# A graph network on one core: messages in 32-column steps, one aggregation matmul per edge attribute, and one product for what a transpose leaves over

## The chip, the cores and the metric

The kernel runs on one core of a Trainium2 chip. The metric is the device time of one execution in microseconds (us). All arithmetic is in 32-bit floats. Each core has a TensorE (PE in the profile), a VectorE (DVE), a ScalarE (ACT), a GpSimd (POOL) and a SyncE (SP), and DMA queues that these engines fill. In this kernel GpSimd issues the gathers of node rows by index, SyncE issues the plain loads, and ScalarE issues the stores of finished node blocks.

## The reference, cut to what matters

Two layers of a graph network run over N = 6250 nodes and E = 200000 edges. A node has 160 features: 64 scalars and 32 vectors of three components. Edges are sorted by the node they end at (`dst`); early nodes have many more edges than late ones.

```python
# layer 0 (w: 192 weights an edge, from 10 inputs an edge; g: the mixed source node's row)
weight = silu(edge_length_embedded @ W_fc1) @ W_fc2
w0, w1, w2, w3 = weight[:, :64], weight[:, 64:128], weight[:, 128:160], weight[:, 160:]
gs, gv = x1s[edge_src], x1v[edge_src]            # 64 scalars; 32 vectors
e_s, e_v = edge_attr[:, :1], edge_attr[:, 1:]    # 4 attributes an edge: 1 + 3
mid0a = w0 * gs * e_s                            # 64
mid0b = w3 * einsum('euc,ec->eu', gv, e_v) / sqrt(3)      # 32
mid1a = w1[:, :, None] * gs[:, :, None] * e_v[:, None, :] # 64 x 3
mid1b = w2[:, :, None] * gv * e_s[:, :, None]             # 32 x 3
agg = segment_sum(concatenate([mid0a, mid0b, mid1a, mid1b]), edge_dst) / 4
# then linear maps of each node's sums, a residual and a layer norm

# layer 1 (w: 224 weights an edge, from 64 inputs an edge)
m_s1 = w1 * es * e0                              # 64
m_s2 = w4 * einsum('eci,ei->ec', ev, e1) / sqrt(3)        # 32
m_v1 = (w2 * es)[:, :, None] * e1[:, None, :]             # 64 x 3
m_v2 = w3[:, :, None] * ev * e0[:, :, None]               # 32 x 3
m_v3 = w5[:, :, None] * cross(ev, e1[:, None, :]) / sqrt(2) # 32 x 3
# segment sums as above, linear maps, silu and gates, a residual and a layer norm
```

Every message is a product of a weight, a gathered feature and one of four edge attributes. So a node's sum can be taken attribute by attribute: for each attribute the products of weights and features (`mid` in the kernel) are multiplied from the left by a matrix that has the attribute in the row of the edge and the column of its node (`sel`).

## The kernel before

**Tiles, groups and units.** 200000 edges are 1563 tiles of 128; two tiles are a pair (782), four a unit (391). Tiles are gathered into 284 groups of 3 to 12, such that the nodes at which a group's edges end lie in a window of 32. One loop over units runs for each layer, in `windows(i, loads, work)`. It is pipelined by hand: in step `u` it issues the gathers of unit `u + 4`, the weights and products of unit `u + 2`, the hidden layer of unit `u + 3`, and the aggregation of unit `u`. TensorE keeps this order as written (`keep_in_program_order`, in the helpers `matmul` and `transpose`, lines 134 and 139, under which every TensorE instruction shows in the profile). The other engines' orders are chosen by a scheduler from the same program.

**Steps of a unit.**
- `gather` (L665): one indirect DMA a tile on GpSimd brings 128 rows of 160 columns from `table` into `g`. A tile of `g` holds a pair, and there are 8 of them. `src`, the indices, and `ea`, the edge attributes, are loaded by SyncE for 48 tiles at a time (L578, L579).
- `inputs` and `hidden`: SyncE loads the edge inputs `e`, in layer 0 for 4 tiles at a time into one of three fixed buffers `e0` to `e2`, in layer 1 for 8 tiles at a time into one of two buffers `e`. TensorE makes `pa` (one matmul of 512 columns in layer 0, of 256 columns in layer 1), ScalarE turns it into `h`.
- `weights`: TensorE makes `pw` from `h`, one matmul a tile. There are three `pw` buffers in PSUM, a pair in each.
- `places` (L699): VectorE makes `sel`, 4 times 32 columns a tile.
- `products` (L681, L686): VectorE multiplies `pw` by `g` into `mid`. A pair takes one operation of 256 elements a partition for the scalars, and one of 192 for each kind of vector message (two in layer 0, three in layer 1). The messages of a tile lie in 320 columns in layer 0, and 416 in layer 1.
- `aggregate`: TensorE adds `sel` times `mid` to `pg`, a PSUM tile with a band of 32 partitions for each of the four attributes. A list `sums` says which columns of `mid` go to which band. In layer 0 there are six matmuls a tile (160, 96, 64, 64, 32 and 32 columns), so that the bands hold 160, 96, 96 and 96 columns. In layer 1 there are seven (160, 64, 96, 128, 96, 64 and 32), and every band holds 160.
- After a group's last tile ScalarE copies `pg` to `r` (L728, L730). One unit later `turn(g)` has TensorE transpose `r` into `pt`, of which there is one buffer, and VectorE adds `pt` to the group's window of `sm` (L749) and `sr` (L751). In layer 1 the 32 columns of `r` beyond 128 are turned by four matmuls of 32 columns against slices of the identity `ident`, ahead of the transpose of the other 128.

**Node blocks.** 49 blocks of 128 nodes are worked on as soon as their groups are turned: `prepare` and `proceed` put one step of such a block into a unit (`second_nodes` in layer 0, `last_nodes` in layer 1). Their matmuls go to `pn`, a PSUM tile with one buffer: the sums in `sm` and `sr` times weights `rm0`, `rr0` in layer 0, `rm1`, `rr1` in layer 1. In layer 1 three of these five matmuls are 96 columns wide, for the attributes 1 to 3. A block of layer 0 ends with four matmuls for layer 1's input, two of them 32 columns wide against `whoz`. Layer 0's blocks write the `table` of layer 1, and `xself` and `xmid`, which layer 1's blocks read back on SyncE.

**Prologue.** Ahead of both layers the kernel loads the nodes, writes layer 0's `table`, subtracts each group's first node from `dst`, and checks that the windows hold (otherwise a slower path, `general`, would run; it does not run with these inputs). It also fills the combined weights: `rm0` with copies on VectorE, `rm1` and `rr1` with 16 loads on SyncE.

Of the kernel before, what the change touches and what calls it, by code (L numbers as in the profile page):

```python
# [86 lines left out]
def kernel(ctx: ExitStack, tc: tile.TileContext, a, out):  # L87
# [17 lines left out]

    nc = tc.nc
# [68 lines left out]
    nc.gpsimd.dma_start(nv[:tail_n, NB - 1, :], a["nv_tail"])  # L175

# [192 lines left out]
    for j in range(2):  # L369
# [3 lines left out]
        for k in range(2):  # L373
# [5 lines left out]
    nc.vector.tensor_copy(rm0[0:64, 1:4, :, S:],  # L379
                          q[0:64, None, :, S:].to_broadcast([64, 3, 2, V]))  # L380
    nc.vector.tensor_copy(rm0[64:96, 1:4, :, 0:S],
                          q[64:96, None, :, 0:S].to_broadcast([32, 3, 2, S]))
# [10 lines left out]
    for at, n, f in ((0, 160, 0.125), (160, 32, r3 / 8), (192, 32, r2 / 8)):  # L393
# [4 lines left out]
    pieces = [(rm1[0:64, 0, ss], l2s[0:64]), (rm1[64:96, 0, vx], l2v[64:96]),  # L398
              (rm1[96:128, 0, vy], l2v[64:96]), (rr1[0:32, vz], l2v[64:96])]
    pieces += [(rr1[32 * c:32 * c + 32, ss], l2s[64:96]) for c in (1, 2, 3)]  # L400
    pieces += [(rm1[0:64, 1 + c, v], l2v[0:64]) for c, v in enumerate((vx, vy, vz))]

    for c, v0, v1 in ((1, vz, vy), (2, vz, vx), (3, vy, vx)):
        pieces += [(rm1[64:96, c, v0], l2v[96:128]), (rm1[96:128, c, v1], l2v[96:128])]
# [3 lines left out]
    for o, f in ((rm1[:, :, 0:96], fs), (rm1[:, :, 96:], fv), (rr1[:, 0:96], fs),  # L408
                 (rr1[:, 96:], fv), (rm1[64:96, 1, vz], -1.0), (rm1[96:128, 2, vx], -1.0),
                 (rm1[64:96, 3, vy], -1.0)):  # L410
        nc.vector.tensor_scalar(o, o, f, None, op0=OP.mult)
# [95 lines left out]
    def last_nodes(b, work, clear):  # L507
# [10 lines left out]
        def summed():  # L518
# [5 lines left out]
            for c in (1, 2, 3):  # L524
                matmul(q[:, 96:192], sm[:, c, rows], rm1[:, c, 96:192], start=False, stop=(c == 3))
# [20 lines left out]
    def windows(i, loads, work):  # L546
        nw = (192, 224)[i]

        at_c, at_d, at_f, at_a, at_b, wid = ((0, 64, None, 160, 224, 320),
                                             (0, 160, 64, 256, 320, 416))[i]  # L550

        if i == 0:
            sums = [(0, at_a, 0, 1, 160, 0), (1, 0, 0, 1, 96, 0), (2, 0, 0, 1, 64, 0),
                    (3, 0, 0, 1, 64, 0), (2, at_d + V, 0, 1, V, 64), (3, at_d + 2 * V, 0, 1, V, 64)]
        else:
            sums = [(0, at_a, 0, 1, 160, 0), (1, 0, 0, 1, 64, 0), (2, 0, 0, 1, 96, 0),
                    (3, 0, 0, 1, 128, 0), (1, at_f + V, 0, 1, 96, 64),
                    (2, at_f + 2 * V, 2 * V, 2, V, 96), (3, at_d + 2 * V, 0, 1, V, 128)]
        made = {}
        ec = (EC // 2, EC)[i]  # L560

        inputs_of = None
        if i == 0:

            inputs_of = [loads.tile([P, EC * P // 2], F32, name=f"e{k}", bufs=1) for k in range(3)]
            for e in inputs_of:
                nc.vector.memset(e, 0.0)
# [24 lines left out]
        def inputs(c):  # L592

            e0 = c * ec * P
            n = min(ec * P, E - e0)
            if i == 0:
                e = inputs_of[c % 3]
                nc.sync.dma_start(e[:10, :n], a["e10"][:, e0:e0 + n])
            else:

                e = loads.tile([P, EC * P // 2], F32, name="e", bufs=2)
# [68 lines left out]
        def products(p):  # L670

            m = min(2, NT - 2 * p)
            n = P if m == 2 else edges_of(2 * p)
            mid = work.tile([P, 2, 416], F32, name="mid", bufs=6)
            q, g = made["w", p], made["g", p]
            o = mid[:n, :m, :wid]
            gs = g[:n, :m, None, 0:S].to_broadcast([n, m, 2, S])
            gv = g[:n, :m, S:D].rearrange("p j (c d) -> p j c d", c=3)
            two = bass.AP(tensor=o.tensor, offset=o.offset,
                          ap=[o.ap[0], o.ap[1], [at_a, 2], [1, S]])  # L680
            nc.vector.tensor_tensor(  # L681
                two, q[:n, :m, 0:2 * S].rearrange("p j (k d) -> p j k d", k=2), gs, OP.mult)
            for w0, at in ((128, at_b), (160, at_d), (192, at_f)):
                if at is None:
                    continue
                nc.vector.tensor_tensor(  # L686
                    o[:, :, at:at + 96].rearrange("p j (c d) -> p j c d", c=3), gv,
                    q[:n, :m, None, w0:w0 + V].to_broadcast([n, m, 3, V]), OP.mult)
            made["m", p] = mid
# [19 lines left out]
        def aggregate(t):  # L709
# [6 lines left out]

            for q, (c, c0, step, k, w, at) in enumerate(sums):
                opens = first and not any(x[0] == c for x in sums[:q])
                closes = last and not any(x[0] == c for x in sums[q + 1:])
                o = mid[:n, t % 2, c0:c0 + w]  # L720
                if k > 1:
                    o = bass.AP(tensor=o.tensor, offset=o.offset, ap=[o.ap[0], [step, k], [1, w]])
                matmul(pg[32 * c:32 * c + 32, at:at + k * w], s[:n, t % 2, c, :], o,
                                 start=opens, stop=closes, tile_position=(0, 32 * c))
            if last:
                r = work.tile([P, 160], F32, name="r")
                w = (96, 160)[i]
                nc.scalar.activation(r[:, :w], pg[:, :w], AF.Copy)  # L728
                if i == 0:
                    nc.scalar.activation(r[:32, 96:], pg[:32, 96:160], AF.Copy)  # L730
                made["r", g] = r

        def turn(g):
# [5 lines left out]
            else:  # L739
                for c in range(4):  # L740
# [249 lines left out]
```

## Time and profile before

| | |
|---|---|
| median of 3 runs | 4143.48 us (4136.02 to 4146.3) |
| the profiled execution | 4137.19 us, of which the profile's span is 4135.4 us |
| granted clock of TensorE, mean | 0.911 |
| TensorE (PE) busy, matmuls | 3570.4 us, 86%, 53817 instructions |
| TensorE weight loads (PEld) | 2582.1 us, 62% |
| VectorE (DVE) busy | 2959.6 us, 72%, 10845 instructions |
| GpSimd (POOL) busy | 3013.5 us, 73%, 3232 instructions |
| ScalarE (ACT) busy | 947.6 us, 23%, 2386 instructions |
| layer 0, from its first gather to the end of its last | 66.9 to 2089.8 us |
| layer 1, the same | 2137.4 to 4101.3 us |

A busy share is an average over both layers, the prologue and the seam between the layers. A matmul's end is modelled, so the busy time of TensorE contains overlap of matmuls in its pipeline. A float32 matmul appears as two instructions, its two passes, each with a weight load of its own (PEld), which runs beside the matmul ahead of it. The rows of a profile name an instruction by source line, engine, operation and tiles; "idle before" is the time in which the engine stood still just ahead of it, with what ended the wait.

### The profile page before, as it was taken

The page shows a single profiled execution, that of the slowest core. Times are in us where ns is not written, and L with a number is a line of the kernel's source. Part 1 is how long each engine was busy: PE and PEld are TensorE (multiplying, and loading weights), DVE is VectorE, ACT ScalarE, POOL GpSimd, SP SyncE. Part 2 cuts the span into 40 slices and gives each one's busy share as a digit, 9 for nine tenths or more (in the row PEclk, how much of TensorE's full clock was granted, in tenths as well). Part 3 has the DMA queues.
Part 4 walks back from the last instruction along what each step waited for, and adds up shares of the span by engine and source line. Part 5 has one row for each costly group of instructions (what it writes and reads, how often), then busy time and mean ns, then how long its engine had stood idle before and what let it go on. Part 6 is the DMA issues. An engine that isn't in the chain of part 4 may idle for free.

```text
span 4135.4 us, 137335 instructions
## 1 busy us (share of the span) xinstructions
PE 3570.4 (86%) x53817; PEld 2582.1 (62%) x53817; DVE 2959.6 (72%) x10845; ACT 947.6 (23%) x2386; POOL 3013.5 (73%) x3232
## 2 busy tenths in 40 slices
PE   7878888889999999999988888888888788888877
PEld 5555566566666666666666666666666566666655
DVE  6766666667677777677657777777777777778887
ACT  2111111222223333333320011111112122222233
POOL 4777777777777777776637777777777777777775
PEclk8999999999999999999988888888898899888898
DMA  4222222332333333322223333333333333333432
GB/s 131 72 73 77 75 78 76 80 80 79 82 82 83 85 81 85 83 79 78 76 60 96 92 101 100 98 97 102 101 97 106 101 105 105 105 105 99 111 107 71
DMA packets 301525, 371.47 MB, mean 90 GB/s; under 512 B 86987, under 2 KB 245212, under 8 KB 300872
## 3 DMA queue, kind: packets, MB, share of 16 engines
q0 software_dynamic: 151056, 257.36, 23.6%
q1 hardware_dynamic: 121192, 88.36, 7.5%
q10 hardware_dynamic: 28624, 16.88, 1.3%
q8 instruction: 430, 7.05, 0.7%
q14 instruction: 223, 1.83, 0.1%
HBM read 341.49 MB, written 20.80 MB: 88 GB/s over the span
## 4 chain that ended last, share of the span: by engine, by line
PE 38%; issue 18%; DMA 17%; POOL 13%; DVE 12%; DVEq 1%; SPq 0%; ACT 0%; POOLq 0%; ACTq 0%
DMA g<-table,src 15%; POOL g L665 13%; PE pw L134 12%; PE pg L134 10%; PE pa L134 7%; PE pn L134 6%; DVE mid L686 4%; DVE sel L699 2%; PE pt L139 2%; DVE mid L681 2%; DMA e<-in_e 1%; PE pn L139 1%; DVE sm L749 1%; DVEq L746 1%; DVE nx L442 1%
## 5 line engine op out<-in xcount | busy, mean ns | idle before, releaser
L665 POOL DMA_INDIRECT g<-table,src x3126 | 2991.9, 957 | 1082.9 <-issue 752.5
L134 PE MATMUL pw<-fc,h 100*128 100x192 f32 (+1 forms) x6252 | 1272.9, 377 | 220.8 <-DVE mid L686 191.3
L134 PEld LDWEIGHTS pg<-mid,sel 128*32 128x32 f32 x40638 | 943.1, 118 | 490.4 <-issue 478.2
L134 PEld LDWEIGHTS pw<-fc,h 100*128 100x128 f32 (+1 forms) x6252 | 941.5, 201 | 380.3 <-issue 206.6
L686 DVE TENSOR_TENSOR mid<-g,pw 128x192 f32<-128x192 f32 x3910 | 1168.6, 346 | 0.0
L681 DVE TENSOR_TENSOR mid<-pw,g 128x256 f32<-128x256 f32 x1564 | 659.5, 422 | 697.4 <-DMA g<-table,src 441.7
L134 PE MATMUL pg<-mid,sel 128*32 128x64 f32 (+4 forms) x40638 | 1144.7, 255 | 0.0
L699 DVE SCALAR_TENSOR_TENSOR sel<-iota,off,ea 128x128 f32<-128x128 f32 x3126 | 956.6, 344 | 189.5 <-PE pg L134 156.9
L134 PE MATMUL pa<-e,fc 128*100 128x512 f32 (+1 forms) x1566 | 737.5, 555 | 117.3 <-DMA e<-in_e 117.0
L624 ACT ACTIVATE h<-pa 100x512 f32<-100x512 f32 x391 | 233.4, 597 | 1059.2 <-PE pa L134 1043.0
L134 PEld LDWEIGHTS pa<-e,fc 128*100 128x100 f32 (+1 forms) x1566 | 263.3, 192 | 247.9 <-issue 131.3
L636 ACT ACTIVATE h<-pa 128x256 f32<-128x256 f32 x392 | 150.0, 383 | 1138.9 <-PE pa L134 1127.3
L139 PE MATMUL pt<-ident,r 128*96 128x128 f32 (+1 forms) x852 | 230.3, 293 | 15.5 <-DVE sr L751 15.5
L749 DVE TENSOR_TENSOR sm<-pt,sm 96x128 f32 (+1 forms) x568 | 162.2, 286 | 106.6 <-PE pt L139 96.1
L728 ACT ACTIVATE r<-pg 128x96 f32<-128x96 f32 (+1 forms) x568 | 155.7, 274 | 360.1 <-PE pg L134 246.9
L139 PEld LDWEIGHTS pt<-ident,r 128*96 128x96 f32 (+1 forms) x852 | 106.4, 125 | 130.5 <-issue 58.7
L134 PE MATMUL pn<-rm,sm 96*128 96x128 f32 (+4 forms) x980 | 155.6, 312 | 17.0 <-DVE sm L749 15.8
L134 PEld LDWEIGHTS pn<-rm,sm 96*128 96x128 f32 (+3 forms) x980 | 148.8, 212 | 24.6 <-DVE sm L749 19.8
L134 PE MATMUL pt<-ident,r 128*32 128x32 f32 x2272 | 86.1, 205 | 56.7 <-DVE sr L751 47.4
L134 PEld LDWEIGHTS pt<-ident,r 128*32 128x32 f32 x2272 | 90.5, 120 | 61.8 <-issue 60.1
L440 ACT ACT_TABLE_LOAD x96 | 123.2, 1283 | 6.3 <-DVE mv L439 4.6
L134 PE MATMUL pn<-rr,sr 64*128 64x128 f32 (+2 forms) x196 | 58.5, 383 | 70.5 <-DVE sr L751 70.5
(132 smaller groups left out, 1227.5 us busy)
## 6 DMA issues: line engine op xcount, KB each, us to landing
g<-table,src POOLq DMA_INDIRECT x3126
e<-in_e SPq DMA_DIRECT2D x781, 64.0 KB
e<-in_e SPq DMA_DIRECT2D x390, 20.0 KB
ea<-in_ea_main SPq DMA_DIRECT2D x63, 96.0 KB
xself<-no ACTq DMA_DIRECT2D x48, 96.0 KB
no<-xself SPq DMA_DIRECT2D x48, 96.0 KB
xg<-in_x_main SPq DMA_DIRECT2D x12, 320.0 KB
table<-rg SPq DMA_DIRECT2D x12, 320.0 KB
```

Of the source, the lines that this page charges most:

```text
L134: r = nc.tensor.matmul(*args, **kw)
L139: r = nc.tensor.transpose(*args)
L440: nc.scalar.activation(mv[:n, 1:2], mv[:n, 1:2], AF.Sqrt, bias=eps[:n])
L442: nc.vector.tensor_scalar(y, y, mv[:n, 0:1], mv[:n, 1:2], op0=OP.subtract, op1=OP.mult)
L624: nc.scalar.activation(h[:100, :n], p[:100, :n], AF.Silu)
L636: nc.scalar.activation(h[:kk, c0:c1], p[:kk, c0:c1], AF.Silu, scale=0.125)
L665: nc.gpsimd.indirect_dma_start(out=g[:n, j, :], out_offset=None, in_=table[i][:, :], in_offset=bass.IndirectOffsetOnAxis(ap=of(t)[0], axis=0))
L681: nc.vector.tensor_tensor(two, q[:n, :m, 0:2 * S].rearrange("p j (k d) -> p j k d", k=2), gs, OP.mult)
L686: nc.vector.tensor_tensor(o[:, :, at:at + 96].rearrange("p j (c d) -> p j c d", c=3), gv, q[:n, :m, None, w0:w0 + V].to_broadcast([n, m, 3 ...
L699: made["last"] = nc.vector.scalar_tensor_tensor(s[:n, j], iota[:n, None, :].to_broadcast([n, 4, W]), w, e[:, :, None].to_broadcast([n, 4, ...
L728: nc.scalar.activation(r[:, :w], pg[:, :w], AF.Copy)
L749: nc.vector.tensor_tensor(sm[:h, :, at], pt[:h, :P].rearrange("p (c w) -> p c w", c=4), sm[:h, :, at], OP.add)
```

## The change

Four things are rearranged together.

1. The columns of `mid` are laid out in places of 32, so that the messages of one attribute lie at a constant step. The list `sums` becomes one entry an attribute (place, step, number of 32-column pieces), and a tile has four aggregation matmuls in both layers, of 160, 96, 96 and 96 columns in layer 0 and of 160 columns each in layer 1. The products are written to these places by a list `kinds`: four operations a pair in layer 0 (two of 128 elements a partition and two of 192), six in layer 1 (128, 128, 192, 128, 64 and 192).
2. In layer 1 the 32 columns that the transpose leaves over are copied by ScalarE into the diagonal 32x32 blocks of one of three tiles `rest`, four copies a group. `turn` then transposes first, and turns the rest with one matmul against `fold` (the identity folded to 32 columns) afterwards.
3. Both layers share the three `e` buffers, which are zeroed before the first layer. Layer 1 had two of its own.
4. The columns of the sums are in another order, so the combined weights `rm0`, `rm1` and `rr1` are filled in other places: nine copies into `rm0` in place of two, 20 loads in place of 16, and in `last_nodes` the matmuls of attributes 1 and 3 are 192 columns wide in place of 96. The path `general` is reordered to match.

```diff
+    fold = const.tile([P, W], F32, name="fold")
+    nc.vector.tensor_reduce(fold, ident.rearrange("p (c w) -> p w c", w=W), AX.X, OP.add)
+    rest = [const.tile([P, P], F32, name=f"rest{k}") for k in range(3)]
+    for t in rest:
+        nc.vector.memset(t, 0.0)
...
-    nc.vector.tensor_copy(rm0[0:64, 1:4, :, S:],
-                          q[0:64, None, :, S:].to_broadcast([64, 3, 2, V]))
-    nc.vector.tensor_copy(rm0[64:96, 1:4, :, 0:S],
-                          q[64:96, None, :, 0:S].to_broadcast([32, 3, 2, S]))
+    for c, at_c, at_d in ((1, (32, 64), 0), (2, (0, 64), 32), (3, (0, 32), 64)):
+        for k, r in enumerate(at_c):
+            nc.vector.tensor_copy(rm0[r:r + 32, c, :, S:], q[32 * k:32 * k + 32, :, S:])
+        nc.vector.tensor_copy(rm0[at_d:at_d + 32, c, :, 0:S], q[64:96, :, 0:S])
...
             for c in (1, 2, 3):
-                matmul(q[:, 96:192], sm[:, c, rows], rm1[:, c, 96:192], start=False, stop=(c == 3))
+                v = slice(96 if c == 2 else 0, 192)
+                matmul(q[:, v], sm[:, c, rows], rm1[:, c, v], start=False, stop=(c == 3))
...
-        at_c, at_d, at_f, at_a, at_b, wid = ((0, 64, None, 160, 224, 320),
-                                             (0, 160, 64, 256, 320, 416))[i]
-        if i == 0:
-            sums = [(0, at_a, 0, 1, 160, 0), (1, 0, 0, 1, 96, 0), (2, 0, 0, 1, 64, 0),
-                    (3, 0, 0, 1, 64, 0), (2, at_d + V, 0, 1, V, 64), (3, at_d + 2 * V, 0, 1, V, 64)]
-        else:
-            sums = [(0, at_a, 0, 1, 160, 0), (1, 0, 0, 1, 64, 0), (2, 0, 0, 1, 96, 0),
-                    (3, 0, 0, 1, 128, 0), (1, at_f + V, 0, 1, 96, 64),
-                    (2, at_f + 2 * V, 2 * V, 2, V, 96), (3, at_d + 2 * V, 0, 1, V, 128)]
+        scalar = lambda w, place: (w, V, 0, 2, place, 2)
+        vector = lambda w, place, step, c=0, n=3: (w, 0, S + c * V, n, place, step)
+        kinds = ((scalar(0, 2), scalar(S, 5), vector(128, 9, 2), vector(160, 0, 3)),
+                 (scalar(0, 2), scalar(S, 10), vector(128, 9, 2), vector(160, 5, 3, 0, 2),
+                  vector(160, 1, 1, 2, 1), vector(192, 0, 3)))[i]
+        sums = (((5, 2, 5), (0, 2, 3), (2, 1, 3), (2, 2, 3)),
+                ((9, 1, 5), (2, 1, 5), (0, 2, 5), (0, 1, 5)))[i]
...
-            if i == 0:
-                e = inputs_of[c % 3]
+            e = inputs_of[c % 3]
...
-                e = loads.tile([P, EC * P // 2], F32, name="e", bufs=2)
...
-            mid = work.tile([P, 2, 416], F32, name="mid", bufs=6)
+            mid = work.tile([P, 2, 14 * V], F32, name="mid", bufs=6)
...
+            def parts(x, at, step, k):
+                u = x[:, :, at:at + V]
+                return bass.AP(tensor=u.tensor, offset=u.offset,
+                               ap=[u.ap[0], u.ap[1], [step, k], [1, V]])
+            for w, w_step, c, k, place, step in kinds:
                 nc.vector.tensor_tensor(
-                    o[:, :, at:at + 96].rearrange("p j (c d) -> p j c d", c=3), gv,
-                    q[:n, :m, None, w0:w0 + V].to_broadcast([n, m, 3, V]), OP.mult)
+                    parts(mid[:n, :m], V * place, V * step, k), parts(g[:n, :m], c, V, k),
+                    parts(q[:n, :m], w, w_step, k), OP.mult)
...
-            for q, (c, c0, step, k, w, at) in enumerate(sums):
...
-                matmul(pg[32 * c:32 * c + 32, at:at + k * w], s[:n, t % 2, c, :], o,
-                                 start=opens, stop=closes, tile_position=(0, 32 * c))
+            for c, (at, step, k) in enumerate(sums):
+                o = mid[:n, t % 2, V * at:V * at + V]
+                o = bass.AP(tensor=o.tensor, offset=o.offset, ap=[o.ap[0], [V * step, k], [1, V]])
+                matmul(pg[32 * c:32 * c + 32, :k * V], s[:n, t % 2, c, :], o,
+                       start=first, stop=last, tile_position=(0, 32 * c))
             if last:
                 r = work.tile([P, 160], F32, name="r")
-                w = (96, 160)[i]
+                w = (96, P)[i]
                 nc.scalar.activation(r[:, :w], pg[:, :w], AF.Copy)
                 if i == 0:
                     nc.scalar.activation(r[:32, 96:], pg[:32, 96:160], AF.Copy)
+                else:
+                    for c in range(4):
+                        k = slice(32 * c, 32 * c + 32)
+                        nc.scalar.activation(rest[g % 3][k, k], pg[k, P:P + V], AF.Copy)
...
-                for c in range(4):
-                    k = slice(32 * c, 32 * c + 32)
-                    matmul(pt[k, P:P + W], r[:, P:P + W], ident[:, k],
-                           start=True, stop=True, tile_position=(0, 32 * c))
                 transpose(pt[:, :P], r[:, :P], ident)
+                matmul(pt[:, P:P + W], rest[g % 3], fold, start=True, stop=True)
...
+            inputs_of = [loads.tile([P, EC * P // 2], F32, name=f"e{k}", bufs=1) for k in range(3)]
+            for e in inputs_of:
+                nc.vector.memset(e, 0.0)
             for i in range(2):
-                windows(i, loads, work)
+                windows(i, loads, work, inputs_of)
```

## The prediction

> **What bounds the kernel now.** I read the busy times by stage first, since shares over the whole span mix stages.
>
> ```profile
> core 0: us, PE busy (x) PEld busy (x) DVE busy (x) ACT busy (x) POOL busy (x), PEclk, DMA share, GB/s
> 1000.00:1200.00 200.00, 181.53 (x2487) 125.25 (x2489) 139.79 (x498) 51.20 (x136) 151.87 (x159) 0.96 0.30 82
> 1800.00:2000.00 200.00, 186.85 (x2366) 130.00 (x2364) 141.65 (x526) 68.89 (x199) 135.16 (x140) 0.99 0.29 78
> 2600.00:2800.00 200.00, 171.84 (x2791) 130.84 (x2790) 144.80 (x524) 27.18 (x67) 151.56 (x160) 0.87 0.36 97
> 3600.00:3800.00 200.00, 163.98 (x3034) 125.72 (x3036) 158.91 (x619) 53.72 (x121) 151.87 (x159) 0.87 0.39 105
> 3800.00:4000.00 200.00, 163.90 (x3209) 124.04 (x3208) 164.76 (x656) 60.97 (x139) 151.57 (x160) 0.91 0.39 105
> ```
>
> The reader is to see POOL's count: 159 or 160 gathers in 200 us almost everywhere, whatever PE does. A gather takes 0.95 us and the next starts 0.30 us later, so 1.25 us each and 5.0 us for a unit of four tiles. 3126 of them are 3908 us of the 4135 us span. PE's 86% is not the bound there. The exception is the end of layer 0, 1600 to 2089 us, where PE is busy for 187 of 200 us and gathers fall to 140.
>
> The second view is the chain of waits, stage by stage (2137 to 2700 us, then 3824 to 4136 us):
>
> ```profile
> by line: issue 37.0%; POOL g L665 36.7%; DMA g<-table,src 24.3%; DVE mid L686 0.9%; DVE sel L699 0.4%; DVE mid L681 0.4%; POOLq L665 0.2%; DVEq L681 0.1%; DVE gate L533 0.0%; DVEq L699 0.0%
> ...
> by line: DVE mid L686 14.8%; PE pw L134 12.4%; PE pg L134 10.6%; issue 8.0%; DVE sel L699 7.5%; PE pn L134 7.2%; DVE mid L681 5.9%; PE pa L134 5.1%; PE pt L139 3.9%; DVE sm L749 2.9%; DVEq L746 2.9%; DMA g<-table,src 2.5%; PE pt L134 2.3%;
> ```
>
> Layer 1 begins as a pure gather queue and ends as a loop of DVE and PE. The waits of DVE say the same: from 3000 to 3200 us it waits 37.7 us for gathers, from 3800 to 4000 us 1.8 us, but then 34 us for PE. The loop falls behind the gathers: the last gather ends at 4101.3 us and the last pair's first product starts at 4115.4 us. That delay of 14 us and what follows it are the path to the end; POOL itself is not stalled, since a gather may run up to eight pairs (20 us) ahead.
>
> Third, the timeline, for what a burst of `pg` matmuls costs:
>
> ```profile
> 1001.08 1.02 PE L134 MATMUL pa<-e,fc 128*100 128x512 f32 x2
> 1002.03 1.27 PE L134 MATMUL pg<-mid,sel 128*32 128x160 f32 x48
> ...
> 1006.80 0.73 PE L134 MATMUL pg<-mid,sel 128*32 128x160 f32 x24
> ...
> 3926.80 1.33 PE L134 MATMUL pg<-mid,sel 128*32 128x160 f32 x56
> ...
> 3927.93 0.42 DVE L681 TENSOR_TENSOR mid<-pw,g 128x256 f32<-128x256 f32 x1
> ...
> 3928.26 0.87 DVE L686 TENSOR_TENSOR mid<-g,pw 128x192 f32<-128x192 f32 x3
> ...
> 4013.27 1.22 PE L134 MATMUL pa<-e,fc 128*128 128x256 f32 x2 [6.41 <-DMA e<-in_e]
> ```
>
> Each f32 matmul is two passes. Two more tiles cost 1.27 - 0.73 = 0.54 us, 135 ns for each of four passes, though six matmuls lie in each tile. The 160 columns of band 0 at the rate of `pa` (its second pass starts 0.43 us after the first, for 512 columns: 0.84 ns each) are 135 ns. So the four bands stream side by side and the burst lasts as long as its longest band.
>
> **The change part by part.**
>
> *Fewer `pg` matmuls.* Layer 0 goes from six to four a tile, layer 1 from seven to four: 7815 matmuls, 15630 passes fewer. Columns by band stay 160, 96, 96, 96 and four times 160. By the row, layer 0 gains nothing, since band 0 had one matmul before. Layer 1 gains at most 1.33 - 1.27 = 0.06 us a unit (56 passes against 48), 23 us of PE in 391 units, nearly all under the gathers. The Trainium skill (TensorEngine Tiling, "Instruction Overhead") says that a matmul costs about 60 cycles however short. Then 64 and 32 columns cost 124 cycles where a joined 96 cost 96; at the 2.4 GHz of its page "Trainium Kernel Development and Optimization" (Quick Reference) 12 ns for each of 16 merged passes a unit in layer 0, 0.19 us, and 17 us over the PE-bound stretch (some 360 gathers from 1600 to 2089 us, 91 units). The trace measures the burst itself, and it has no room for that: I take 0. Strided operands: shapes with two pieces of 32 columns occur among the 64-column matmuls, whose mean is 236 ns between 201 (32) and 268 (96), so I take nothing for five pieces; a cost would show as a burst over 1.33 us.
>
> *More products on DVE.* A pair had three operations in layer 0 and four in layer 1, now four and six on the same elements: 782 + 1564 = 2346 more. Back to back, 256 elements take 0.33 us to the next start and 192 take 0.267; that is 67 ns fixed and 1.04 ns an element. So a pair gets 0.067 us longer in layer 0 and 0.133 in layer 1 (1.13 to 1.27 us), a unit 0.13 and 0.27, all of it 52 + 104 = 156 us of DVE. The skill (VectorE: DVE Perf Modes, the section on the TRN2 errata) speaks harder against this: 120 cycles fixed with a PSUM source, 125 ns each at 0.96 GHz, 293 us in all and 0.5 us a unit in layer 1. The trace's 67 ns decides. Where gathers bound, DVE has waits for them as cover (37.7 us in 200, against 10.8 added). Gathers are not slowed by it in what the trace shows: at DVE 145 or 165 of 200 us they come at the same pace. In the PE-bound stretch of layer 0, DVE waits for PE (28 us before `mid`, 26 before `sel`, 24 before `sm` in 380 us), which covers 0.13 a unit; PE's own waits for DVE there (13 us on `sr`, 6 on `nx`, 6 on `sm`) might grow: +1.5 us, between 0 and 91 x 0.13 = 12.
>
> From 3600 us on the cover is gone. DVE's 158.9 and 31 us of waits for others than gathers leave 10 us there; 164.8 and 34 leave 1.8 after 3800. What of 0.27 us a unit is on the loop lies between 0 (DVE's waits for PE shrink by as much) and all. One of two pairs stands between `pw` and the `sm` for which the next turn waits, so I take 0.14, and 0.06 more for the two parts below: 0.2. At 4006 us the chain is on a gather again, so the loop had caught up; of the 36 units from 3824 to there 7 us are added, and I keep 3 for what is not caught up. The 22 units behind it add 4.5.
>
> *Turn and rest (layer 1).* Before: four 32-column products, then the transpose, 0.20 + 0.26 us to the next matmul. Now the transpose, then one product with 128 columns of weights. Its nearest row is the `whoz` group, four passes of 32 columns in 0.56 us to the next start: 0.28 for two. So 0.54 against 0.46 us, 284 x 0.08 = 23 us of PE, which takes back what `pg` gave. In the changed order `sr` has no wait of its own, so `sm` stands behind the product too, 0.1 us later; `sr`, and the next turn behind it (one `pt` buffer), wait with it. Four 32x32 copies a group are new on ACT: nearest is L730, 199 ns, 0.15 apart back to back, so 0.6 us a group and 170 us in all, on an engine busy for 61 of 200 us at most there. Queued behind them is `h`, needed a unit later; the turn that reads `rest` comes a unit later too, and three buffers cover it.
>
> *Wider `pn` in layer 1.* Two of five matmuls go from 96 to 192 columns: 2 x 2 passes x 96 x 0.84 = 0.32 us a block, 16 us in 49 blocks; three blocks lie after the last gather: +1 us.
>
> *Three `e` buffers for both layers.* An `e` load can start two units earlier in layer 1. The 6.41 us stall at 4013 us is such a load behind an `src` load on SP, which itself waited for a buffer. It sits on the path after 4006. Gain between 0 and 6.4, and the changed order of SP has some of those loads ahead of `src`: I take -5. What is lost: layer 1's first loads no longer go out at 72 us, but wait for layer 0's last `pa` (2102 us); they stand ahead of the blocked `xself` loads, and layer 1's first `pa` is at 2133: 0.
>
> *Prologue.* Seven more copies into `rm0` (six of 64 elements, three of 128 instead of two large ones, +1.3 us), `fold`, three memsets, four more loads on SP, which there waits 17 us for rows to write. The first gather at 66.9 us follows the last table write (63.0 us) by 3.9 us; at the layers' seam the same step is 4.2. So the write, not DVE, seems to release it: +0.5, at most 1.5.
>
> Sum: 0.5 + 1.5 + 3 + 4.5 - 5 + 1 for `pn` + 1 for six turns and the copies in the tail = +6.5 us. On the profiled execution's own 4137.2 us (span 4135.4) this is 4143.7; it stood 6.3 under the median of the runs, so 4150.
>
> **The rivals.**
> *DVE takes over at the end of layer 1 (slower).* Its waits for PE stay as they are and 0.27 us a unit all counts: 200 us of gathers then need 158.9 + 31 + 10.8 = 201 us after 3600 and 164.8 + 34 + 10.8 = 210 after 3800. That is +1, +10, +6 to 4115, 2 in the tail, 4 for turns and `pn`, nothing gained on `e`: +23, 4167. It decides once DVE's unit, 4.12 us busy and 0.85 waiting for PE, passes 5.0. For it: PE clock is 0.87 to 0.91 here and bursts take 2.36 us after idle PE, so longer waits feed on themselves. Against: the loop caught up by 4006.
> *PE gains from fewer matmuls (faster).* The 17 us of the rule above in layer 0, and the whole 8.7 us of two `e` stalls: 4150 - 21 = 4129. Against it stands 135 ns for 160 columns.
> *Nothing shows:* all of DVE's work hides and `e` gives its 5 us: about 4143.
>
> **How the numbers follow.** A difference under 0.3%, 12.4 us, can't be told from none with this kernel. The likeliest case, a few us either way of 4150 with its own range of 4138 to 4155, has 0.34; "nothing shows" 0.08: together the 0.42 of no change. The slower rival has 0.33. Another 0.12 is its upper part, with layer 0's 12 us and the full price of turns, or longer DVE waits that lower the clock: up to 4190. The faster one has 0.13. The range of 4120 to 4190 leaves out the deepest part of the faster case and a slower one fed further by the clock.
>
> **What would show it.** `pg` bursts of 1.2 to 1.3 us for 32 passes in both layers; pairs of 0.93 and 1.27 us on DVE; 159 to 160 gathers per 200 us to 4000; no `e` stall at 4013; last product 12 to 18 us after the last gather. A burst under 1.2 us in layer 0, or gathers below 157 in 200 us before 3900, would make it wrong.

## The result and the profile after

| | before | after |
|---|---|---|
| median of 20 runs, us | 4138.45 (4132.11 to 4152.51) | 4160.57 (4141.76 to 4168.68) |
| ratio, with its 95% interval | | 1.0043 (1.0033 to 1.0053) |
| span of the profiled execution, us | 4135.4 | 4155.1 |
| granted clock of TensorE, mean | 0.911 | 0.916 |

The changed kernel is slower by 0.43%, some 18 us by the ratio (the medians are 22.1 us apart), although it has 17334 TensorE matmul instructions fewer. The mean clock is no lower than before; the clock of the stage that matters is taken up below.

The busy times by stage, in the same five stretches as before:

```profile
core 0: us, PE busy (x) PEld busy (x) DVE busy (x) ACT busy (x) POOL busy (x), PEclk, DMA share, GB/s
1000.00:1200.00 200.00, 185.68 (x1876) 125.18 (x1875) 142.95 (x576) 52.96 (x139) 152.48 (x157) 0.96 0.30 80
1800.00:2000.00 200.00, 189.65 (x1792) 129.10 (x1791) 142.30 (x588) 68.89 (x199) 139.25 (x142) 0.97 0.29 78
2600.00:2800.00 200.00, 172.90 (x1748) 117.38 (x1752) 155.81 (x684) 34.94 (x121) 151.27 (x161) 0.87 0.36 96
3600.00:3800.00 200.00, 172.74 (x1822) 126.34 (x1826) 165.05 (x764) 76.58 (x283) 151.66 (x158) 0.87 0.38 103
3800.00:4000.00 200.00, 161.12 (x1813) 112.84 (x1807) 168.17 (x776) 87.88 (x329) 151.33 (x159) 0.89 0.39 105
```

From 3800 us VectorE is busy for 168.2 of 200 us. POOL (GpSimd) still starts 158 and 159 gathers in 200 us in the last two rows, nearly the gather pace of 160. TensorE has 24% to 44% fewer instructions than before in these five rows and about the same busy time. In the last row its granted clock is 0.89, before 0.91. The kernel with the four matmuls alone (below) also has 0.89 there and loses nothing in layer 1, so the clock is not the reason.

The chain of waits from 3824 us to the end, sums by line:

```profile
by line: DVE mid L690 22.4%; PE pw L135 13.8%; PE pg L135 9.3%; PE pn L135 8.7%; issue 6.7%; DVE sel L703 6.0%; PE pa L135 5.9%; PE pt L140 3.6%; DVE sm L750 2.5%; ACT L454 2.3%; DMA g<-table,src 2.1%; PE pt L135 2.1%; DVE sr L752 2.1%; DVE
```

The six products (L690) now carry 22.4% of it; before, the two lines of products (L681 and L686) had 20.7% together. The waits of VectorE from 3800 to 4000 us, in total, number and longest:

```profile
engine line waited for: us in total, times, longest us
DVE sm L750 <- PE pt L135: 12.1, 16, 1.3
DVE mid L690 <- PE pw L135: 9.4, 13, 0.9
DVE no L541 <- PE pn L135: 7.3, 8, 1.0
DVE mv L455 <- ACT mv L454: 1.4, 4, 0.5
DVE mid L690 <- DMA g<-table,src: 0.6, 1, 0.6
```

Before, in the same stretch:

```profile
DVE sm L749 <- PE pt L139: 18.3, 20, 3.3
DVE mid L681 <- PE pw L134: 8.5, 13, 0.9
DVE no L526 <- PE pn L134: 4.9, 9, 0.6
DVE mid L681 <- DMA g<-table,src: 1.8, 1, 1.8
DVE sm L749 <- PE pt L134: 0.9, 1, 0.9
DVE sm L749 <- PE pw L134: 0.4, 1, 0.4
```

Waits for a gather are the slack of VectorE: the extra products can use them up. They were down to 1.8 of 34.8 us before and are 0.6 of 30.8 us now; the rest are waits for other work, nearly all of it TensorE's. With the 168.2 us of work they fill the 200 us. TensorE on its side waits 50.5 us for `sr` in 310 us; before it was 30.1 us in 290:

```profile
engine line waited for: us in total, times, longest us
PE pt L140 <- DVE sr L752: 50.5, 20, 3.1
PE pn L135 <- DVE sr L752: 8.9, 13, 1.4
PE pw L135 <- ACT h L643: 0.5, 2, 0.3
```

So each of the two waits for the other, and extra time of the products can add to this loop; the experiments test whether it does. No wait for `e` is left in that list, which is whole. How far the products are behind is read from the last gather and the first product of the last pair, in the timeline of the kernel before and then of the changed one:

```profile
4100.33 1.01 POOL L665 DMA_INDIRECT g<-table,src  x1 [0.30 <-DVE mid L686]
...
4115.38 0.27 DVE L681 TENSOR_TENSOR mid<-pw,g 64x128 f32<-64x128 f32 x1
```

```profile
4114.62 0.90 POOL L672 DMA_INDIRECT g<-table,src  x1 [0.30 <-DVE sel L703]
...
4133.70 0.90 DVE L690 TENSOR_TENSOR mid<-g,pw 64x64 f32<-64x64 f32 x6
```

Before, the product starts 14.0 us after the gather's end, now 18.2 us. The gather itself ends 14.2 us later: gathers may run only eight pairs ahead, so products that are late hold the gathers back too.

The timeline of the changed kernel at full clock, for the price of its new parts:

```profile
3903.56 1.29 PE L135 MATMUL pg<-mid,sel 128*32 128x160 f32 x32
3904.78 0.33 PE L140 MATMUL pt<-ident,r 128*128 128x128 f32 x1
3904.95 0.31 PE L135 MATMUL pt<-fold,rest 128*128 128x32 f32 x2
3905.18 1.03 PE L135 MATMUL pw<-fc,h 64*128 64x224 f32 x8
...
3924.93 1.34 DVE L690 TENSOR_TENSOR mid<-g,pw 128x128 f32<-128x128 f32 x6
```

```profile
1000.59 1.27 PE L135 MATMUL pg<-mid,sel 128*32 128x160 f32 x32
1001.79 1.75 PE L135 MATMUL pn<-rm,sm 96*128 96x192 f32 x12
```

A unit's burst takes 1.22 us to the next instruction in layer 1 with 32 passes (1.26 with 56 before) and 1.20 us in layer 0 (1.20 with 48). A turn takes 0.40 us of TensorE from one start to the next. Six products take 1.34 us to their end and 1.25 to the next start of VectorE (3926.18 us).

### The profile page after: what moved, and what is told of

It is laid out like the page before. It is cut to its first block, busy times and chain, and to the rows that moved or that the text cites. A ratio compares the mean times of both kernels' runs of the same rounds, so it can differ in the third digit from the quotient of the medians.

```text
span 4155.1 us, 106324 instructions
## 1 busy us (share of the span) xinstructions
PE 3625.3 (87%) x36483; PEld 2479.3 (60%) x36483; DVE 3099.3 (75%) x13202; ACT 1120.5 (27%) x3524; POOL 3025.7 (73%) x3232
## 4 chain that ended last, share of the span: by engine, by line
PE 32%; issue 21%; POOL 16%; DMA 15%; DVE 12%; ACT 2%; DVEq 1%; SPq 0%; POOLq 0%; ACTq 0%
POOL g L672 16%; DMA g<-table,src 14%; PE pw L135 10%; DVE mid L690 8%; PE pg L135 7%; PE pn L135 6%; PE pa L135 6%; PE pt L140 2%; DVE sel L703 1%; DMA e<-in_e 1%; DVE sm L750 1%; DVEq L747 1%; PE pn L140 1%; ACT L631 1%; ACT L454 0%
## 5 line engine op out<-in xcount | busy, mean ns | idle before, releaser
L690 DVE TENSOR_TENSOR mid<-g,pw 128x128 f32<-128x128 f32 (+2 forms) x7820 | 1856.3, 302 | 665.9 <-DMA g<-table,src 416.7
L135 PE MATMUL pw<-fc,h 100*128 100x192 f32 (+1 forms) x6252 | 1306.5, 376 | 241.9 <-DVE mid L690 224.0
L135 PEld LDWEIGHTS pw<-fc,h 100*128 100x128 f32 (+1 forms) x6252 | 965.8, 200 | 433.1 <-issue 266.1
L135 PE MATMUL pg<-mid,sel 128*32 128x160 f32 (+1 forms) x25008 | 1125.8, 304 | 0.1
L135 PEld LDWEIGHTS pg<-mid,sel 128*32 128x32 f32 x25008 | 756.9, 116 | 552.9 <-issue 476.2
L734 ACT ACTIVATE rest<-pg 32x32 f32<-32x32 f32 x1136 | 209.1, 184 | 12.5
L135 PE MATMUL pn<-rm,sm 96*128 96x128 f32 (+4 forms) x980 | 177.3, 336 | 21.0 <-DVE sm L750 19.8
L135 PEld LDWEIGHTS pn<-rm,sm 96*128 96x128 f32 (+3 forms) x980 | 161.9, 218 | 29.0 <-DVE sm L750 23.5
L135 PEld LDWEIGHTS pt<-fold,rest 128*128 128x128 f32 x568 | 112.9, 242 | 0.0
L752 DVE TENSOR_TENSOR sr<-pt,sr 64x32 f32 (+1 forms) x568 | 101.5, 179 | 0.6 <-DVE sm L750 0.4
```

Source lines behind the costliest of these rows:

```text
L135: r = nc.tensor.matmul(*args, **kw)
L690: nc.vector.tensor_tensor(parts(mid[:n, :m], V * place, V * step, k), parts(g[:n, :m], c, V, k), parts(q[:n, :m], w, w_step, k), OP.mult)
L734: nc.scalar.activation(rest[g % 3][k, k], pg[k, P:P + V], AF.Copy)
L752: made["last"] = nc.vector.tensor_tensor(sr[:k, at], pt[:k, P:P + W], sr[:k, at], OP.add)
```

## The experiments

Each kernel was timed beside the kernel before on the same chip. The ratio stands with its 95% interval; "layer 1" is the time in that kernel's profile from the first gather of layer 1 to the `sel` of its last tile (1977.8 us before, 1992.7 after). Four kernels with the products and the two `e` buffers of before, in three different orders of VectorE's instructions, took 1977.4 to 1978.7 us there, so this stretch repeats well. It is read from one profile of each kernel. Layer 0 doesn't: in kernels that don't change it, it took 2025 to 2040 us.

**The products alone.** In the kernel before, each pair's product of 256 elements becomes two of 128, and in layer 1 one product of 192 becomes 128 and 64. Nothing else is edited.

```diff
...
-            nc.vector.tensor_tensor(
-                two, q[:n, :m, 0:2 * S].rearrange("p j (k d) -> p j k d", k=2), gs, OP.mult)
+            for k in range(2):
+                nc.vector.tensor_tensor(two[k], q[:n, :m, k * S:k * S + S],
+                                        g[:n, :m, 0:S], OP.mult)
...
+                for c0, c1 in (((0, 2), (2, 3)) if i == 1 and w0 == 160 else ((0, 3),)):
...
```

> The kernel before with nothing changed but the products on VectorE: four operations a pair in layer 0 and six in layer 1, as in the changed kernel, written to the old places of mid. Theory A (VectorE's extra operations close a loop of VectorE and TensorE at the end of layer 1, and that is the change's cost): 12 to 20 us slower than before, a ratio of 1.003 to 1.005, with the lag of products behind gathers rising from about 3700 us to 12 us or more, and the last product 16 to 19 us behind the last gather. Theory B (the turn with four copies and a product behind the transpose is the cost): within 5 us of before.

Measured: 1.0044 (1.0030 to 1.0059), the median 16.3 us above before; layer 1 took 1990.0 us, and the last pair's product started 19.4 us behind the last gather. That is as much as the loss of the whole change.

**The matmuls alone.** The kernel before with four entries in `sums` for each layer. They have the widths of the change but read other columns of `mid`, so this kernel does the work without giving the right sums. Layer 1's part of the edit:

```diff
...
-            sums = [(0, at_a, 0, 1, 160, 0), (1, 0, 0, 1, 64, 0), (2, 0, 0, 1, 96, 0),
-                    (3, 0, 0, 1, 128, 0), (1, at_f + V, 0, 1, 96, 64),
-                    (2, at_f + 2 * V, 2 * V, 2, V, 96), (3, at_d + 2 * V, 0, 1, V, 128)]
+            sums = [(0, at_a, 0, 1, 160, 0), (1, 0, V, 5, V, 0), (2, 0, 2 * V, 5, V, 0),
+                    (3, 0, V, 5, V, 0)]
```

> The kernel before with four aggregation matmuls a tile (columns by band as before: 160, 96, 96, 96 and four times 160) on strided or wrong columns of mid, so that sums of attributes 1 to 3 are taken over other columns; all else as before. The prediction's reading (a burst lasts as long as its longest band): within 4 us of before, bursts of a unit 1.20 us to the next start in layer 0 and 1.21 to 1.23 in layer 1 against 1.26. The rival that each matmul has a fixed price: 10 to 25 us faster, with shorter bursts in layer 0.

Measured: 1.0021 (1.0013 to 1.0029), slower by 8.9 us. Neither reading said that. The bursts were as expected (1.20 us in layer 0, 1.22 in layer 1), so the price of the matmuls is right, and something else made the loss. The scheduler had given VectorE another order: between the products, `sel`, `sm` and `nx` stood elsewhere in some 180 places. Layer 1 took 1977.4 us, so the loss lies ahead of it.

**The old turn.** The changed kernel with the old turn:

```diff
-                w = (96, P)[i]
+                w = (96, 160)[i]
...
-                transpose(pt[:, :P], r[:, :P], ident)
-                matmul(pt[:, P:P + W], rest[g % 3], fold, start=True, stop=True)
+                for c in range(4):
+                    k = slice(32 * c, 32 * c + 32)
+                    matmul(pt[k, P:P + W], r[:, P:P + W], ident[:, k],
+                           start=True, stop=True, tile_position=(0, 32 * c))
+                transpose(pt[:, :P], r[:, :P], ident)
```

> The changed kernel with the old turn of layer 1: one copy of 160 columns on ScalarE, four 32-column matmuls, then the transpose; everything else as changed. Theory A: 14 to 20 us slower than before, that is 0 to 5 us faster than the changed kernel. Theory B: within 6 us of before.

Measured: 1.0048 (1.0033 to 1.0063). The old turn gives nothing back that can be seen (the changed kernel has 1.0033 to 1.0053): the copies on ScalarE and the product against `fold` are not the loss.

**The buffers alone.** The kernel before with three shared `e` buffers.

```diff
...
+            e = inputs_of[c % 3]
...
-                e = loads.tile([P, EC * P // 2], F32, name="e", bufs=2)
...
```

> The kernel before with the three e buffers for both layers, all else as before. The prediction: 0 to 6 us faster than before, the stall of 6.4 us for e near 4013 us gone, and layer 1's first product no later. Rival (the seam is lost by the shared buffers): 2 to 6 us slower, with the first gather of layer 1 or its first hidden layer later.

Measured: 0.9993 (0.9982 to 1.0003), the median 4.1 us lower, which the interval doesn't tell from none. The scheduler left VectorE's order as it was. The profile shows the mechanism: layer 1 took 1970.6 us. Of the waits of TensorE from 3800 to 4090 us, the longest three of the kernel before and then of this one, the wait for `e` is gone, and no other changes by more than 1.5 us (the one for `mv` is 4.4 us before):

```profile
engine line waited for: us in total, times, longest us
PE pt L134 <- DVE sr L751: 30.1, 14, 3.9
PE pn L134 <- DVE sr L751: 9.4, 13, 1.4
PE pa L134 <- DMA e<-in_e: 8.6, 2, 6.4
```

```profile
engine line waited for: us in total, times, longest us
PE pt L134 <- DVE sr L744: 30.3, 15, 2.8
PE pn L134 <- DVE sr L744: 10.9, 11, 4.1
PE pt L134 <- DVE mv L441: 5.7, 4, 1.5
```

**Work or order?** Splitting the products had also changed the scheduler's order, in some 340 places of VectorE. So the next three kernels hold the order of VectorE, ScalarE and SyncE to a given list, with an edge from each instruction to the next that orders them without a wait.

```diff
+        for en, text in ORDER.items():
...
+            seq = [ran[k + s] for k, s in enumerate(steps)]
...
+            for one, two in zip(seq, seq[1:]):
+                tc.add_manual_dep(two, one.name, mybir.DependencyInfo(
+                    mybir.DependencyClass.NoSync, mybir.DependencyReason.DATA), reason="order")
```

The split products in the order of before:

> The kernel before with the products split (four operations a pair in layer 0, six in layer 1), and with the order of VectorE, ScalarE and SyncE held to that of the kernel before. The scheduler had moved other instructions of VectorE when the products were split. If the operations' own time is the cost: 12 to 20 us slower than before, as with the split alone. If the scheduler's other order is the cost: within 5 us of before.

Measured: 1.0047 (1.0034 to 1.0060); layer 1 took 1992.0 us.

The products of before in the order of the split kernel:

> The kernel before with its own three and four products a pair, in the order of VectorE, ScalarE and SyncE that the scheduler gave to the kernel with split products. If the operations' own time is the cost: within 5 us of before. If the other order is the cost: 12 to 20 us slower.

Measured: 1.0006 (0.9997 to 1.0015), with equal medians. So the operations' own time is the cost, and that order costs nothing that can be seen.

The four matmuls alone, again on other columns of `mid`, in the order of before:

> The kernel with four aggregation matmuls a tile (on other columns of mid, as in that run), and with the order of VectorE, ScalarE and SyncE held to that of the kernel before. That run was 8.6 us slower than before, though its bursts were no longer. If the scheduler's other order made that loss: within 4 us of before. If something in the matmuls themselves does: 6 to 12 us slower again.

Measured: 1.0005 (0.9998 to 1.0011). The loss of the matmuls alone came with the scheduler's order, not with the matmuls: with the order held, 7815 matmuls fewer are worth nothing either way.

**Fewer products.** In layer 1 `mid` is laid out so that the three kinds of vector message stand 96 columns apart, and one operation a tile makes all three. The weights `rm1` and `rr1` are filled to match, and one `pn` matmul is 192 columns wide.

```diff
...
+                for j in range(m):
+                    u = o[:, j, at_b:]
+                    nc.vector.tensor_tensor(
+                        bass.AP(tensor=u.tensor, offset=u.offset,
+                                ap=[u.ap[0], [-96, 3], [V, 3], [1, V]]),
+                        gv[:, j, None, :, :].to_broadcast([n, 3, 3, V]),
+                        q[:n, j, 128:224].rearrange("p (k d) -> p k d", k=3)
+                        [:, :, None, :].to_broadcast([n, 3, 3, V]), OP.mult)
```

> The kernel before with fewer products in layer 1: the three operations of 192 elements a pair become two of 288, one a tile, on the same elements (three operations a pair in place of four). If the number of VectorE operations is the price: 0.067 us a pair less, 0.13 us a unit, and 4 to 9 us faster than before, gained after 3600 us. If the loop at the end of layer 1 is not held by VectorE: within 3 us of before.

Measured: 0.9989 (0.9979 to 0.9999), the median 6.9 us lower; layer 1 took 1971.0 us. This points the other way as well: fewer operations, less time. The order was not held here, and VectorE's other instructions stand elsewhere in some 100 places. In the runs above another order left layer 1 within 1977.4 to 1978.7 us, so its 1971.0 us speaks for the operations; the 0.11% of the whole kernel is less certain.

**Which layer?** The split in layer 1 alone, with the order of before. Against the split kernel the edit is:

```diff
-            for k in range(2):
+            if i == 0:
+                nc.vector.tensor_tensor(
+                    two, q[:n, :m, 0:2 * S].rearrange("p j (k d) -> p j k d", k=2), gs, OP.mult)
+            for k in range(2) if i == 1 else ():
```

> The kernel before with the products split in layer 1 alone (six operations a pair, layer 0 keeps three), in the order of VectorE, ScalarE and SyncE of the kernel before. If the whole price lies at the end of layer 1, as the stages of the profiles say: 14 to 20 us slower than before, as with both layers split. If layer 0 bears its share: 6 to 12 us slower.

Measured: 1.0029 (1.0020 to 1.0038), 11.5 us, at the upper end of the 6 to 12 us expected if layer 0 bears a share. But its layer 1 took 1993.2 us, as long as with both layers split. So layer 1 is the larger part. Whether the other 7 us are layer 0's is not settled: the two intervals overlap (0.20 to 0.38% here, 0.34 to 0.60% with both), and layer 0 differs by more than that from profile to profile.

**Twice the dose.** Eight products a pair in layer 1: all four operations in two, the order held. Against the run before, the edit is:

```diff
-                for c0, c1 in (((0, 2), (2, 3)) if i == 1 and w0 == 160 else ((0, 3),)):
+                for c0, c1 in (((0, 2), (2, 3)) if i == 1 else ((0, 3),)):
```

> The kernel before with eight products a pair in layer 1 (each of the four operations in two), layer 0 and the order as before: 0.53 us a unit more on VectorE where six products were 0.27. If VectorE holds the loop from the point where its cover is used up, the price grows faster than the count, since that point comes earlier: 35 to 60 us slower than before. If each operation has one fixed price on the path: twice the price of six, 28 to 40 us.

Measured: 1.0074 (1.0057 to 1.0092), 31.4 us, and layer 1 took 2010.2 us. By the median this is the second expectation, twice the price; the interval, 24 to 38 us, reaches into both. Against the 11.5 us of six products this is 2.7 times the price for twice the operations; by layer 1's profile (32.4 against 15.4 us) it is 2.1 times, so which of the two forms of growth holds stays open. The stages show VectorE at its limit, and now POOL below the gather pace:

```profile
core 0: us, PE busy (x) PEld busy (x) DVE busy (x) ACT busy (x) POOL busy (x), PEclk, DMA share, GB/s
3600.00:3800.00 200.00, 163.69 (x2948) 124.81 (x2948) 171.77 (x905) 53.14 (x119) 152.18 (x158) 0.89 0.38 103
3800.00:4000.00 200.00, 158.35 (x2907) 118.72 (x2907) 170.82 (x896) 53.73 (x124) 145.72 (x153) 0.87 0.38 102
```

153 gathers in the second row, 85.4% of VectorE busy.

**The rest of the change.** The changed kernel with four products a pair in layer 1, its order held. They are written to places for which the sums are not made, so the work is done without the right sums.

```diff
+            if i == 1:
+                o = mid[:n, :m]
+                nc.vector.tensor_tensor(
+                    o[:, :, 0:2 * S].rearrange("p j (k d) -> p j k d", k=2),
+                    q[:n, :m, 0:2 * S].rearrange("p j (k d) -> p j k d", k=2),
+                    g[:n, :m, None, 0:S].to_broadcast([n, m, 2, S]), OP.mult)
+                for w, at in ((128, 256), (160, 128), (192, 352)):
...
-            for w, w_step, c, k, place, step in kinds:
+            for w, w_step, c, k, place, step in kinds if i == 0 else ():
```

> The changed kernel with the products of layer 1 in four operations a pair again, written to places of mid for which the sums are not made (the sums of layer 1 are taken over other columns), in the order of VectorE, ScalarE and SyncE of the changed kernel. So it is the change without its extra operations in layer 1. If these are the whole cost: within 6 us of before. If the turn with four copies, the wider matmuls or the prologue cost something: 6 to 12 us slower.

Measured: 1.0006 (0.9995 to 1.0018); layer 1 took 1974.5 us. With layer 1's two extra operations a pair gone, no loss can be told. The interval reaches to 7 us, and the `e` buffers' gain is in it, so a few us from the other parts, layer 0's split among them, are not excluded.

**A version that beats both.** The joined products with the three `e` buffers (VectorE's order as in the joined kernel, so not that of before).

> The kernel before with three products a pair in layer 1 and with the three e buffers for both layers. Both took about 7 us off layer 1 in the profiles. If the two gains are at different points of the path: 8 to 14 us faster than before. If both only shorten the same lag behind the last gather: 5 to 8 us faster.

Measured: 0.9975 (0.9965 to 0.9985), the median 11.7 us below before; layer 1 took 1967.7 us. Its stages:

```profile
core 0: us, PE busy (x) PEld busy (x) DVE busy (x) ACT busy (x) POOL busy (x), PEclk, DMA share, GB/s
3600.00:3800.00 200.00, 161.23 (x3098) 123.35 (x3098) 156.82 (x551) 55.12 (x123) 151.58 (x160) 0.90 0.40 107
3800.00:4000.00 200.00, 164.16 (x3155) 123.93 (x3159) 159.44 (x572) 59.83 (x136) 151.56 (x160) 0.91 0.38 104
```

160 gathers in both rows. The last pair's product starts 6.7 us after the last gather's end, where it was 14.0 before.

How far the first product of a pair starts behind the end of its second gather, in us, the mean over the pairs whose product starts in the stretch, from the trace of each:

| stretch | 3700 to 3800 | 3800 to 3900 | 3900 to 4000 | 4000 to 4090 |
|---|---|---|---|---|
| joined, three `e` (3 a pair) | 3.2 | 4.1 | 4.1 | 3.4 |
| before, three `e` (4) | 3.7 | 4.3 | 4.3 | 5.5 |
| before (4) | 3.6 | 7.0 | 6.0 | 9.6 |
| after (6) | 4.0 | 8.3 | 13.1 | 16.4 |
| split in layer 1 (6) | 4.8 | 9.5 | 14.3 | 16.4 |
| eight | 4.4 | 12.8 | 16.6 | 17.1 |

The lag rises only from 3750 us on, in all kernels with more products. It stops at 17 to 20 us, which is the eight pairs of `g`; from there the gathers themselves come late.

## Why the prediction was right, and where it was not

The range of 4120 to 4190 holds the 4160.6. The mechanism that came is not the likeliest case, no change to be told (0.42), but the rival "DVE takes over at the end of layer 1", in its lower part: it was worked out as +23, and the ratio gives +18. The prediction's own sum, +6.5 us, is about a third of that. That its 4150 lies only 10 us below the result is in part luck: it stood on a median of 4143.5 from three runs of the kernel before, and twenty runs gave 4138.5.

**Fewer `pg` matmuls: right.** The sum took 0 against 17 us of gain by the rule of a fixed price for each matmul. (The 17 us counted one cycle a column. At the prediction's own 0.84 ns a column and 2.4 GHz a column is two cycles, so 32 columns are already over the rule's 60, and worked out so it promised nothing either.) The bursts in layer 0 are 1.20 us with 32 passes as with 48, in layer 1 1.22 against 1.26, and with the order held the four matmuls alone are at 1.0005. Strided pieces of 32 columns cost nothing that shows. The rival "PE gains" is out.

**More products: the size of one was right, the number of units was not.** Six products were put at 1.27 us from start to start; from 3924.93 us it is 1.25. What failed is the step "at 4006 us the chain is on a gather again, so the loop had caught up": the sum kept 3 us of the 36 units ahead of 4006, and 4.5 of the 22 behind. The reading of the kernel before was right: by its trace the lag of the product behind its gather is back at 2.0 us at 4009 us. But that catching up was not carried over to the changed kernel, where the lag does not fall below 14.9 us from 4000 to 4050 us. The 1.8 us of waits for gathers in 200 were too little cover for 0.27 us a unit, 10.8 in 200, and nothing is given back. (The waits for PE in that row are 33.0 us, not the 34 that the prediction took.) The 0.2 us a unit on the loop is near what came: from 3750 us, where the lag begins to rise, to 4115 us there are 73 units, 14.6 us, and layer 1 is 14.9 us longer. As the start is chosen from the result, this is a fit and no test.

**Three `e` buffers: the mechanism was right, the sum counted it twice over.** The stall is gone, and alone the buffers take 7.2 us off layer 1's profile and some 3 us off the runs, which can't be told from none. But in the changed kernel VectorE is what TensorE waits for, and a stall of TensorE for `e` would probably have been covered by that. With the old turn and three buffers layer 1 took 1988.3 us, with the split alone and two buffers 1990.0 to 1993.2; the gap of 7 us without the split is only 2 to 5 here. These are single profiles, and no run sets two buffers into the changed kernel, so this is argued and not shown. If it holds, the -5 belonged to the case in which VectorE has slack, and not into the sum.

**Turn and rest: wrong in sign, and small.** The `whoz` row gave 0.54 us; a turn takes 0.40, less than the 0.46 before. The four copies take 0.74 us a group on the mean, not 0.6 (209 us in all), on an engine that had room for it. The run without the new turn is not faster.

**Layer 0, prologue, `pn`:** +1.5, +0.5 and +1 can't be told in these runs. Layer 0's part may be nearer to 7 us, the difference between the split in both layers and in layer 1 alone, which lies within the bound of 12 that the prediction gave; this stays open. The first gather starts at 68.0 us, 1.1 us later than before; in other kernels with an unchanged prologue it lies between 65.1 and 69.8.

**"Gathers are not slowed": right for layer 1, perhaps not for layer 0.** Where gathers bound layer 1 they take as long as before; in layer 0 they are some 8 ns longer each. The last section has the numbers.

**The signs.** Bursts, the six products and the missing stall came as written. Gathers were 158 and 159 in 200 us from 3600 us on, and the last product came 18.2 us after the last gather, at the edge of the 12 to 18 given.

## What to carry to other kernels

An engine that is busy for 80% of a stage may have no slack if it also waits 15% of the time on a partner that waits for it in turn. Before calling an extra operation hidden, add the busy time, those waits and the new work, and compare the sum with the period of the stage. Here the prediction had done this sum (201 and 210 us for 200), and set it aside because the loop had once caught up. Fixed costs of many small operations count there (67 ns each by the rows of before), so merging operations on the engine of the loop gained more than merging matmuls that stream side by side. A gain and a loss that lie on the same loop need not add. Where a scheduler orders the instructions, an edit is worth comparing with the order held as well, since the order alone moved one kernel by 0.16%.

## What the runs showed of the hardware

In these profiles the gathers on GpSimd are slightly longer where VectorE has more products beside them. From 2150 to 3640 us, in layer 1, the gathers of the kernel before (first row) and of the kernel with eight products (second), each with its busy time and number:

```profile
2150.00:3640.00 1490.00, 1128.69 (x1187) 0.87 0.37 100
```

```profile
2150.00:3640.00 1490.00, 1129.91 (x1183) 0.89 0.37 100
```

That is 950.9 and 955.1 ns a gather, 5 us over the stretch. The eight kernels with three or four products have 948.6 to 950.9 ns there, the five with six products 950.9 (the changed kernel) to 953.9.

From 68 to 1450 us, in layer 0, the kernel before and the changed kernel:

```profile
68.00:1450.00 1382.00, 1048.03 (x1096) 0.94 0.30 79
```

```profile
68.00:1450.00 1382.00, 1050.32 (x1089) 0.95 0.29 78
```

That is 956.2 and 964.5 ns, and seven gathers fewer. The five kernels with four products in layer 0 have 959.1 to 965.3 ns, the nine with three 954.9 to 961.1, so the ranges overlap. In the changed kernel layer 0's last gather ends at 2086.3 us all the same, before at 2089.8; so the delay is made up later in the layer. Each figure is from one profile. Why the gathers are longer is not shown here.
